# Last steps of a sequence spread over the loop in two attention layers, and a product moved on GpSimd in a state-space layer

## The chip, the cores and the metric

The kernel runs on one core of a Trainium2 chip. Its time is device time in microseconds (us) of one execution of the whole program. Before the change the median of three runs is 2588.48 us (2585.68 to 2595.79). The engines are named as in the profile: PE is TensorE's matrix multiplication and PEld its weight loads, DVE is VectorE, ACT is ScalarE, POOL is GpSimd, SP is SyncE, which here only issues transfers.

## The reference, cut to what matters

A decoder of four layers works on x of shape (16, 128, 256): 16 sequences of 128 rows with 256 features. Each layer adds an attention (or state-space) step, a cross attention to a context, and a feed-forward step, each on the layer-normalised x. The change touches three of the twelve steps:

```python
# layer 1, cross attention: heads are groups of features, q and k are normalised along the features
qn = _l2norm(qh, axis=-2); kn = _l2norm(kh, axis=-2)            # 8 heads of 16 features, 256 "positions"
sm = jax.nn.softmax(5.0 * jnp.einsum('bhdq,bhdk->bhqk', qn, kn), axis=-1)
out = jnp.einsum('bhqk,bhdk->bhdq', sm, vh).reshape(B, Dv, Tq)

# layer 2, state-space in chunks of 32 steps, 32 heads of 16, state 128
y = (Y_diag + Y_off).reshape(b, nc * CHUNK, HEADS, HEAD_DIM) + D[None, None, :, None] * xs
y = y * silu(gate); y = y * rsqrt(mean(y * y) + EPS) * norm_w
return y @ out_proj_w.T

# layer 3, attention: 16 heads of 16, causal with a bias that falls with the distance
attn = jax.nn.softmax(q @ k / 4 + alibi, axis=-1)
return (attn @ v) @ Wo.T

# in the decoder
x = x + _L1_xattn_ref(_layernorm(x), ctx, ctx)
x = x + _L2_attn_ref(_layernorm(x), ...)
x = x + _L3_attn_ref(_layernorm(x), ...)
```

## The kernel before

x stays in on-chip memory for the whole program. The 16 sequences are worked through in four groups of four (g is the group, j the sequence in it, b = 4g + j). Instructions are written in Python in the order of the loops, and a scheduler then orders them on each engine by their dependences and its own estimate of times; each engine works through its own list strictly in that order. The order in the text is therefore a wish and not the order on the engines. `issue_after(i)` forbids the scheduler to put the instructions of its block ahead of instruction i on i's engine.

PSUM, where TensorE writes, is divided into three pools of 512-column buffers: four for scores and projections (`psum`), two for transposes and the like (`psum_t`), two for accumulated results (`psum_a`). A buffer is free again when its last reader is done.

**Layer 1 cross attention** (L693 to L834). `unit(g)` prepares a group in steps: norms (pn, L737), their square roots, and for each sequence a spread of them over the rows (pb, L750) from which qn, kn and the masked queries qb are made. `attend` goes through a group's sequences, each in two half steps (e = 0, 1). A half step makes eight score products ps (L769), each of 32 rows, so that four of them stand in different row groups of TensorE; they are recorded as sixteen. Four exponentials on ScalarE (L775) follow. The product with the values, `mix` (L784), is put off by one half step through the list `late`, so that it doesn't wait for the exponentials. After the second half step's `mix`, `close` ends the sequence in one go: oT is copied out of PSUM (L802, VectorE), turned by four transposes pqT (L807), the reciprocal of the sums rd (L810) and the weighted o (L814) are made on VectorE, two transposes poT (L821) turn it back, and it is added to x (L157). Between half steps one step of the next group's `unit` is issued, and two pieces of `ternary`, which rounds layer 2's feed-forward weights on VectorE (L1468 to L1491) and has no other relation to this step. These pieces stand behind the latest copy of oT by `issue_after`.

**Layer 2 state-space** (`mamba` with `blocks`). For every sequence `begin` transposes the convolved input xc into px (L1110) and copies it to xs, alternately by ScalarE (L89) and VectorE (L91). GpSimd then multiplies xc in place by the skip's factor D (L1113), and makes three scaled copies xw of xs (L1141) for the products poff (L1147), from which yo (L1149) comes. `parts` makes xdp on GpSimd (L1157), transposes yo (pyo, L1161), adds it to the scaled xc (L1163), and makes the products py (L1176) with mt (L1169). `gate` (L1192 to L1197) multiplies by the gate and sums squares; `out` (L1205 to L1209) normalises and projects. GpSimd's queue holds L1113, L1141, L1157, L1193, L1196, L1197 and L1205 of neighbouring sequences.

**Layer 3 attention** (L1530 to L1645). Per sequence: four scores ps (L1584), to each a bias (L1588) and the negative maximum (L1592) on VectorE, the subtraction on GpSimd (L1593), the exponential on ScalarE (L1594). `mix`, one sequence later through `late`, transposes the sixteen heads' weights (ppT, L1602), copies them (L1604) and multiplies with the values (po, L1609), and copies the result to oT (L1614). `close`, one sequence after that through `later`, transposes oT (pqT, L1626), divides by the sums (rd L1629, o L1631), transposes o (pt, L250), copies it (oo, L89 and L91), multiplies with Wo (pa, L97) and adds it to x (L157).

Of the kernel before, what the change touches and what calls it, by code (L numbers as in the profile page):

```python
# [17 lines left out]
ALU = mybir.AluOpType  # L18
# [4 lines left out]
P = 128  # L23
NB = 16
S = 128
# [16 lines left out]
class Decoder:  # L42
# [86 lines left out]
    class Pipe:  # L129
# [8 lines left out]
        def step(self):  # L138
            for d in self.due:
                d[0] -= 1  # L140
            now = [w for n, w in self.due if n <= 0]
            self.due = [d for d in self.due if d[0] > 0]
            for w in now:
                w()
# [548 lines left out]
    def L1_xattn(self):  # L693
        nc = self.nc
        H, d = 8, 16
        with ExitStack() as es:
# [58 lines left out]
                    yield  # L755

            late, units, copies = [], {}, []
            ternary = self.ternary_parts(tn)

            def attend(g, ahead):  # L760
                v, kn, qb = units.pop(g)
                for j in range(GB):
                    b, state = g * GB + j, {}
                    for e in range(2):
                        ps = [self.psum("ps") for r in range(4)]
                        for c in range(2):
                            for r in range(4):
                                rw = slice(32 * r, 32 * r + 32)
                                nc.tensor.matmul(  # L769
                                    ps[r][:, D * c : D * c + D], kn[rw, j, self.cols(c)], qb[rw, j, e], start=True, stop=True  # L770
                                )
                        got = []
                        for r in range(4):
                            pT = big.tile([P, 2, D], F32, tag="pT", name="pT")
                            nc.scalar.activation(pT.rearrange("p c t -> p (c t)"), ps[r], AF.Exp, scale=5.0)  # L775
                            got.append(pT)

                        def mix(j=j, b=b, e=e, got=got, state=state, v=v):
                            if e == 0:
                                state["po"] = self.psum_a("po")  # L780
                            po = state["po"]
                            for c in range(2):
                                for r in range(4):
                                    nc.tensor.matmul(  # L784
                                        po[32 * r : 32 * r + 32, D * e : D * e + D], v[:, j, c, 2 * r + e, :],
                                        got[r][:, c, :], start=(c == 0), stop=(c == 1),
                                    )
                            if e == 1:
                                close(b, po)

                        for f in late:
                            f()
                        late[:] = [mix]
                        next(ahead, None)
                        if copies:
                            with self.tc.issue_after(copies[-1].ins):
                                for _ in range(2):
                                    next(ternary, None)

            def close(b, po):  # L800
                oT = sm.tile([P, 512], F32, tag="oT", name="oT")
                copies.append(nc.vector.tensor_copy(oT, po))  # L802
                pt = self.psum_t("pqT")
                for a in range(2):
                    for e in range(2):
                        at = D * e + P * a
                        nc.tensor.transpose(pt[:, self.cols(2 * a + e)], oT[:, at : at + P], self.ident)  # L807
                pv = pt.rearrange("p (n x) -> p n x", x=32)
                rd = sm.tile([P, 2 * H], F32, tag="rd", name="rd")
                nc.vector.reciprocal(rd, pv[:, :, d])  # L810
                o = sm.tile([P, 2, P], F32, tag="o", name="o")
                for a in range(2):
                    ar = slice(H * a, H * a + H)
                    nc.vector.tensor_tensor(  # L814
                        o[:, a].rearrange("p (r e d) -> p e r d", r=4, e=2),
                        pv[:, ar, 0:d].rearrange("p (e r) d -> p e r d", e=2),
                        rd[:, ar].rearrange("p (e r) -> p e r", e=2).unsqueeze(3).broadcast_to([P, 2, 4, d]), ALU.mult,
                    )
                pb = self.psum_t("poT")
                for a in range(2):  # L820
                    nc.tensor.transpose(pb[:, self.cols(a)], o[:, a, :], self.ident)  # L821
                self.add_x(b, pb[:, :D])
# [3 lines left out]
            for g in range(NG):  # L826
                ahead = unit(g + 1) if g + 1 < NG else iter(())
                attend(g, ahead)
                for _ in ahead:
                    pass  # L830
            for f in late:
                f()
            for _ in ternary:
                pass  # L834

# [126 lines left out]
    def mamba(self, L, H, N, clip):  # L962
# [3 lines left out]
        nc = self.nc  # L966
        HD, Q = 512 // H, 32
        blocks = H == 32
# [8 lines left out]
        with ExitStack() as es:  # L977
# [128 lines left out]
            def begin(g, j, bc_, sz, xc, dt, a, xy):  # L1106
                b = g * GB + j
                pt = self.psum_t("px")
                for c in range(4):
                    nc.tensor.transpose(pt[:, self.cols(c)], xc[:, c, j, :], self.ident)  # L1110
                xs = sm.tile([P, 512], F32, tag="xs", name="xs")
                self.evac(xs, pt)
                nc.gpsimd.tensor_tensor(  # L1113
                    xc[:, :, j, :], xc[:, :, j, :], nw[:, 1, :].unsqueeze(2).broadcast_to([P, 4, S]), ALU.mult
                )
                pg = self.psum_t("pg")
                nc.tensor.matmul(pg[:, :P], bc_[:N, 0, self.cols(j)], bc_[:N, 1, self.cols(j)], start=True, stop=True)
                gm = sm.tile([P, P], F32, tag="gm", name="gm")
                nc.vector.tensor_tensor(gm, pg[:, :P], upto, ALU.mult)
                dj = dt[:, j, :].unsqueeze(2).broadcast_to([P, H, HD])  # L1120
                lcs = []
                if (g, j) not in steps_of:
                    steps(g, j)
                for rb in steps_of.pop((g, j)):
                    ps = self.psum("pseg")
                    nc.tensor.matmul(ps, after, rb.rearrange("p h l -> p (h l)"), start=True, stop=True)
                    lc = ps if blocks else big.tile([P, 512], F32, tag="lc", name="lc")
                    nc.scalar.activation(lc, ps, AF.Exp)
                    lcs.append(lc.rearrange("p (h l) -> p h l", h=per))
                if not blocks:  # L1130
                    xd = sm.tile([P, 512], F32, tag="xd", name="xd")
                    nc.gpsimd.tensor_tensor(heads(xd), heads(xs), dj, ALU.mult)
                    pipe.put(2, lambda: whole(g, j, gm, lcs[0], xd, sz, xc))
                    return lambda: None
                xd = xds[b % 2]
                gf = sm.tile([P, P], F32, tag="gf", name="gf")
                nc.vector.tensor_tensor(gf, pg[:, :P], prior, ALU.mult)
                pf, n, xws = self.psum("poff"), 3 * Q, []
                for c in range(3):
                    xw = big.tile([P, 512], F32, tag="xw", name="xw", bufs=4)  # L1140
                    nc.gpsimd.tensor_tensor(  # L1141
                        heads(xw)[:n], heads(xs)[:n], xy[:n, c, j, :].unsqueeze(2).broadcast_to([n, H, HD]), ALU.mult
                    )
                    xws.append(xw)
                for c in range(4):
                    to = slice(Q * c, Q * c + Q)
                    nc.tensor.matmul(pf[to], gf[:n, to], xws[max(c - 1, 0)][:n], start=True, stop=True)  # L1147
                yo = sm.tile([P, 512], F32, tag="yo", name="yo")
                nc.vector.tensor_tensor(  # L1149
                    heads(yo), heads(pf), xy[:, 3, j, :].unsqueeze(2).broadcast_to([P, H, HD]), ALU.mult  # L1150
                )
                return lambda: parts(g, j, gm, lcs, xd, dj, yo, xs, sz, xc)
# [377 lines left out]
    def L3_attn(self):  # L1530
        nc = self.nc
# [3 lines left out]
        with ExitStack() as es:  # L1535
# [87 lines left out]
            def close(b, oT):  # L1623
                pt = self.psum_t("pqT")
                for n in range(4):
# [6 lines left out]
                    o.rearrange("p (r n d) -> p n r d", r=4, n=4), pv[:, :, 0:d].rearrange("p (n r) d -> p n r d", n=4),  # L1632
                    rd.rearrange("p (n r) -> p n r", n=4).unsqueeze(3).broadcast_to([P, 4, 4, d]), ALU.mult,
                )
                oo = sm.tile([P, 2, P], F32, tag="oo", name="oo")
                self.transpose_rows(oo, [o])
                pa = self.psum_a()
# [1 line left out]
                self.add_x(b, pa[:, :D])  # L1639

            self.overlap(NG, project, attend)
            for q in (later, late, later):
                for f in list(q):
                    q.remove(f)
                    f()  # L1645
# [375 lines left out]
```

## Time and profile before

| what | value |
|---|---|
| median of three runs | 2588.48 us |
| the profiled execution | 2586.49 us, its span 2584.8 us |
| layer 1 cross attention, about 733 to 903.5 us of the span | 170.5 us |
| layer 2 state-space, about 1087 to 1391 us | 304 us |
| layer 3 attention, about 1926 to 2128 us | 202 us |
| scores of layer 1's cross attention, L769, 512 records | 85.4 us busy |
| exponentials there, L775, 128 | 67.6 us busy, 601 ns each |
| skip's product, L1113, 32 in both state-space layers | 33.8 us busy, 1057 ns each |
| subtraction of the maxima in layer 3, L1593, 64 | 65.2 us busy, 1038 ns each |

A record of the profile is one instruction on one engine with its start and length; a matmul on 4-byte numbers is recorded as two. "Idle before, releaser" names what the engine waited for. The granted clock is the share of TensorE's full clock that it had in a stretch; in this profile it is 0.50 or 1.00 at any moment, and a mean over a longer window lies between. Neighbouring matmuls overlap, so the busy time of a line is the time that its records cover together.

### The profile page before, as it was taken

The numbers are of one execution on the slowest core, as the hardware profiler recorded it, in microseconds if no ns is written. First come the engines' busy times: TensorE is split into PE (matmuls) and PEld (weight loads), VectorE is DVE, ScalarE is ACT, GpSimd is POOL, SyncE is SP. The second block draws the span as 40 slices with busy tenths as digits, with TensorE's granted clock in tenths as the row PEclk, the third lists the DMA queues.
The fourth block names the chain that finished last, engine by engine and source line by source line (L and its number), as shares of the span: only waits on it lengthen the run. The fifth ranks groups of instructions, "written<-read, shape, count | busy, mean of one in ns | idle before, by whom it ended". The sixth has DMA issues, their size and how long they took to land. (4 is left out here: it accounts for less than half of the span.)

```text
span 2584.8 us, 33315 instructions
## 1 busy us (share of the span) xinstructions
PE 2283.6 (88%) x12494; PEld 1419.7 (55%) x12510; DVE 1589.0 (61%) x3395; ACT 956.2 (37%) x1726; POOL 949.5 (37%) x983
## 2 busy tenths in 40 slices
PE   7889899889988989989889799898888987699998
PEld 4654454446644445644445465564555555577776
DVE  7996865476756687778887666664465556211110
ACT  1124545355444423344332433345434442112121
POOL 5720102223431142144546866746443333112122
PEclk9987879999977899989889999999999997899999
DMA  4000010000111000100010000000000002233221
GB/s 137 1 29 26 21 58 6 1 25 3 40 41 33 24 1 3 44 1 1 1 29 8 1 1 5 29 34 1 1 29 1 15 32 89 97 87 99 64 71 19
DMA packets 61086, 77.79 MB, mean 30 GB/s; under 512 B 8851, under 2 KB 50579, under 8 KB 60820
## 3 DMA queue, kind: packets, MB, share of 16 engines
q1 hardware_dynamic: 53604, 66.57, 8.0%
q0 software_dynamic: 6784, 8.48, 1.9%
q8 instruction: 101, 1.65, 0.3%
q14 instruction: 69, 0.57, 0.1%
q10 hardware_dynamic: 528, 0.52, 0.1%
HBM read 56.88 MB, written 18.67 MB: 29 GB/s over the span
## 5 line engine op out<-in xcount | busy, mean ns | idle before, releaser
L1897 POOL DMA_INDIRECT out_dram<-y,to x40 | 60.9, 1523 | 301.5 <-ACT y L1896 301.5
L1888 DVE TENSOR_TENSOR hT<-sl,pgb 128x288 f32<-128x288 f32 x112 | 50.6, 454 | 147.7 <-PE pgb L97 147.6
L97 PE MATMUL pga<-xeT,e_w1T 128*128 128x288 f32 x448 | 128.3, 409 | 0.0
L97 PE MATMUL pgb<-xeT,e_w3T 128*128 128x288 f32 x448 | 127.2, 407 | 1.0 <-DVE hT L1888 1.0
L97 PE MATMUL pa<-e_w2T,hT 128*128 128x256 f32 (+1 forms) x560 | 124.5, 380 | 0.0
L97 PEld LDWEIGHTS pa<-e_w2T,hT 128*128 128x128 f32 (+1 forms) x560 | 99.2, 179 | 22.1 <-issue 3.0
L1593 POOL TENSOR_TENSOR sc<-sc,mx 128x512 f32<-128x512 f32 x64 | 65.2, 1038 | 121.7 <-DVE mx L1592 79.5
L1887 ACT ACTIVATE sl<-pga 128x288 f32<-128x288 f32 x112 | 45.9, 410 | 168.5 <-PE pga L97 168.4
L1357 ACT ACTIVATE sc<-sc 128x512 f32<-128x512 f32 x64 | 40.3, 630 | 165.5 <-POOL sc L1356 165.5
L775 ACT ACTIVATE pT<-ps 128x512 f32<-128x512 f32 x128 | 67.6, 601 | 90.0 <-PE ps L769 86.1
L97 PEld LDWEIGHTS pgb<-xeT,e_w3T 128*128 128x128 f32 x448 | 84.9, 190 | 25.2 <-DVE hT L1888 2.0
L214 DVE TENSOR_SCALAR xn<-x,mv,rs 128x256 f32<-128x256 f32 x176 | 86.0, 533 | 20.6 <-POOL rs L107 20.6
L97 PEld LDWEIGHTS pga<-xeT,e_w1T 128*128 128x128 f32 x448 | 84.8, 191 | 23.4
L419 PE MATMUL ps<-qb,kT 32*128 32x512 f32 x256 | 90.6, 795 | 7.8 <-ACT pT L424 4.7
L618 POOL TENSOR_TENSOR rest<-h,h 128x512 f32<-128x512 f32 (+1 forms) x56 | 66.0, 1180 | 74.2 <-ACT h L617 71.8
L201 POOL COPY rs<-mv 128x4 f32<-128x4 f32 x46 | 10.1, 219 | 223.5 <-DVE mv L199 215.7
L424 ACT ACTIVATE pT<-ps 128x512 f32<-128x512 f32 x128 | 68.2, 605 | 61.8 <-PE ps L419 61.7
L1113 POOL TENSOR_TENSOR xc<-xc,nw 128x512 f32<-128x512 f32 x32 | 33.8, 1057 | 153.5 <-PE px L1110 133.9
L198 DVE BATCH_NORM_STATS2 st<-x 128x6 f32<-128x256 f32 x192 | 78.1, 414 | 16.9 <-POOL x L461 10.1
L461 POOL TENSOR_TENSOR x<-x,o 128x256 f32<-128x256 f32 x16 | 16.4, 1028 | 194.7 <-DVE o L457 194.7
L769 PE MATMUL ps<-qb,kn 32*128 32x256 f32 x512 | 85.4, 522 | 1.7 <-ACT pT L775 1.7
L622 DVE TENSOR_TENSOR h<-rest,h 128x512 bf16<-128x512 f32 (+1 forms) x56 | 40.5, 724 | 75.1 <-ACT h L621 75.1
(499 smaller groups left out, 6075.0 us busy)
## 6 DMA issues: line engine op xcount, KB each, us to landing
e_w1T<-in_L_w1T SPq DMA_DIRECT2D x8, 896.0 KB, 6.2
e_w3T<-in_L_w3T SPq DMA_DIRECT2D x8, 896.0 KB
e_w2T<-in_L_w2T SPq DMA_DIRECT2D x8, 896.0 KB
xe<-slots SPq DMA_DIRECT2D x8, 652.5 KB
slots<-blank SPq DMA_DIRECT2D x6, 783.0 KB, 12.7
x<-in_x SPq DMA_DIRECT2D x4, 512.0 KB
ctx<-in_ctx SPq DMA_DIRECT2D x16, 128.0 KB
raw<-in_L_wgu SPq DMA_DIRECT2D x4, 512.0 KB
```

The costliest lines, as they stand in the source:

```text
L97: self.nc.tensor.matmul(out, a, b, start=(i == 0), stop=(i == n - 1))
L198: nc.vector.bn_stats(st[:, j, :], self.x[:, g * GB + j, :])
L214: nc.vector.tensor_scalar(xn[:, j, :], self.x[:, g * GB + j, :], mv[:, j, 0:1], rs[:, j : j + 1], ALU.subtract, ALU.mult)
L419: nc.tensor.matmul(ps[r], kT[rw, j, c, :], qb[rw, j, c].rearrange("p e n -> p (e n)"), start=True, stop=True)
L424: nc.scalar.activation(pT.rearrange("p e n -> p (e n)"), ps[r], AF.Exp, scale=d**-0.5)
L618: engines[0].tensor_tensor(r, t, a, ALU.subtract)
L769: nc.tensor.matmul(ps[r][:, D * c : D * c + D], kn[rw, j, self.cols(c)], qb[rw, j, e], start=True, stop=True)
L775: nc.scalar.activation(pT.rearrange("p c t -> p (c t)"), ps[r], AF.Exp, scale=5.0)
L1593: nc.gpsimd.tensor_tensor(sc, sc, mx.unsqueeze(2).broadcast_to([P, 4, S]), ALU.add)
L1887: nc.scalar.activation(sl, pa[:, :HALF], AF.Silu)
L1888: nc.vector.tensor_tensor(hT[:, f, hs], sl, pb[:, :HALF], ALU.mult)
L1897: i = nc.gpsimd.indirect_dma_start(out, bass.IndirectOffsetOnAxis(to[:m, t : t + 1], 0), y[:m], None, bounds_check=NB * S - 1, oob_is_err= ...
```

## The change

In layer 1's cross attention `close` is cut into three. It now only copies oT and puts `weigh` (pqT, rd, o) into `late`, which puts `turn` (poT and the sum into x) into `late` in its turn. `late` is emptied once in each half step by `step`, which runs only what was there when it began; so the three parts are issued in three half steps following each other. At the end `step` is called until the list is empty.

In layer 3's attention `close` is cut in two in the same way: `expand` (the transposes of o, the product with Wo and the sum into x) goes into `later` and is issued one sequence later. The last emptying of the lists has one round more.

In layer 2's state-space step the product with the skip's factor becomes a function `skip`. With `blocks` (layer 2) it is issued after the three xw, and `issue_after` forbids the scheduler to put it ahead of the third. Layer 1's state-space step issues it where it stood.

```diff
@@ layer 1 cross attention
             late, units, copies = [], {}, []
+
+            def step():
+                for f in list(late):
+                    late.remove(f)
+                    f()
+
@@
-                        for f in late:
-                            f()
-                        late[:] = [mix]
+                        step()
+                        late.append(mix)
                         next(ahead, None)
@@ def close(b, po)
                 oT = sm.tile([P, 512], F32, tag="oT", name="oT")
                 copies.append(nc.vector.tensor_copy(oT, po))
+                late.append(lambda: weigh(b, oT))
+
+            def weigh(b, oT):
                 pt = self.psum_t("pqT")
...
+                late.append(lambda: turn(b, o))
+
+            def turn(b, o):
                 pb = self.psum_t("poT")
...
-            for f in late:
-                f()
+            while late:
+                step()
@@ state-space, begin
-                nc.gpsimd.tensor_tensor(
-                    xc[:, :, j, :], xc[:, :, j, :], nw[:, 1, :].unsqueeze(2).broadcast_to([P, 4, S]), ALU.mult
-                )
+                def skip():
+                    nc.gpsimd.tensor_tensor(
+                        xc[:, :, j, :], xc[:, :, j, :], nw[:, 1, :].unsqueeze(2).broadcast_to([P, 4, S]), ALU.mult
+                    )
+
+                if not blocks:
+                    skip()
@@
-                    nc.gpsimd.tensor_tensor(
+                    last = nc.gpsimd.tensor_tensor(
                         heads(xw)[:n], heads(xs)[:n], xy[:n, c, j, :].unsqueeze(2).broadcast_to([n, H, HD]), ALU.mult
                     )
                     xws.append(xw)
+                with self.tc.issue_after(last.ins):
+                    skip()
@@ layer 3 attention, close
+                later.append(lambda: expand(b, o))
+
+            def expand(b, o):
                 oo = sm.tile([P, 2, P], F32, tag="oo", name="oo")
                 self.transpose_rows(oo, [o])
...
-            for q in (later, late, later):
+            for q in (later, late, later, later):
```

## The prediction

> **What bounds the kernel now.** I read the page first, then sums by window for the three stages that the change touches, then windows laid on the clock's own steps, the order of time inside one sequence, and the waits by stage. The page gives TensorE as the busiest engine, and its clock row is not flat:
>
> ```profile
> PE 2283.6 (88%) x12494; PEld 1419.7 (55%) x12510; DVE 1589.0 (61%) x3395; ACT 956.2 (37%) x1726; POOL 949.5 (37%) x983
> ...
> PEclk9987879999977899989889999999999997899999
> ```
>
> The three stages, in columns of window, length, busy time of PE, PEld, DVE, ACT and POOL, granted clock, DMA share and GB/s:
>
> ```profile
> 733.00:903.50 170.50, 155.53 (x1174) 78.22 (x1173) 110.10 (x232) 80.83 (x141) 23.44 (x29) 0.77 0.10 34
> 1087.00:1391.00 304.00, 261.31 (x1818) 136.74 (x1820) 243.71 (x455) 115.78 (x167) 144.17 (x170) 0.92 0.03 8
> 1926.00:2128.00 202.00, 176.90 (x1140) 102.10 (x1141) 121.15 (x247) 96.40 (x176) 70.04 (x78) 0.94 0.03 11
> ```
>
> Layer 1's cross attention (the first) keeps TensorE busy 91% of the time, but at 0.77 of its clock; the other two have 0.92 and 0.94. What idle does there is seen in windows of the clock's own step, 3.41 us (length, PE busy, granted clock):
>
> ```profile
> 753.73:757.15 3.42, 3.14 (x36) 1.00 0.00 0
> 757.15:760.56 3.41, 2.35 (x22) 1.00 0.00 0
> 760.56:763.97 3.41, 3.41 (x25) 0.50 0.02 5
> ...
> 842.48:845.89 3.41, 2.41 (x29) 1.00 0.00 1
> 845.89:849.30 3.41, 3.41 (x17) 0.50 0.39 126
> ```
>
> A window with 3.14 us of work keeps the clock at 1.00; one with 2.35 or 2.41 (69 to 71%) is followed by half the clock. In this stage the six drops to half follow windows busy 0.69 to 0.78 of their length; every window above 0.8 held the clock, and three below 0.8 did too. So a hole of 1 us costs itself, and then windows at half speed: 78.8 of the 170.5 us run at 0.50 with no hole in them (78.3 busy), and 91.7 us at 1.00 with 14.5 us of holes. Inside one sequence:
>
> ```profile
> 812.73 1.07 PE L784 MATMUL po<-pT,va 128*32 128x256 f32 x16
> 813.73 0.70 PE L769 MATMUL ps<-qb,kn 32*128 32x256 f32 x4
> 814.61 0.66 PE L807 MATMUL pqT<-ident,oT 128*128 128x128 f32 x4 [0.18 <-DVE oT L802]
> 815.20 0.71 PE L769 MATMUL ps<-qb,kn 32*128 32x256 f32 x8
> 816.67 0.33 PE L821 MATMUL poT<-ident,o 128*128 128x128 f32 x1 [0.76 <-DVE o L814]
> ```
>
> The ends of a sequence (pqT, poT) stand inside the next scores, each waiting for VectorE, and they cut the sixteen score records into pieces. The waits, stage by stage (us, times, longest):
>
> ```profile
> PE poT L821 <- DVE o L814: 8.0, 11, 1.1
> PE pqT L807 <- DVE oT L802: 5.2, 10, 1.5
> ...
> POOL xw L1141 <- DVE xs L91: 24.8, 8, 4.0
> PE poff L1147 <- POOL xw L1141: 19.2, 16, 2.4
> ...
> PE pa L97 <- ACT oo L89: 6.2, 15, 1.3
> PE pqT L1626 <- ACT oT L1614: 5.3, 5, 1.3
> ```
>
> **Layer 1 cross attention.** No instruction is added or removed. In the built program's order a half step becomes "16 score records, pqT or poT, 16 po records, at times one pb". So oT has the whole next scores as cover (1.15 us in one piece, where the clock is full) against a copy of 0.69, and o has pqT to poT, 1.07 + 1.15 us and 0.55 more with a pb, against rd 0.25 and o 0.48.
> (a) Holes: 8.0 + 5.2 = 13.2, less the last sequence's 0.78 + 0.77, which has nothing to stand behind: 11.7. What is late next is VectorE's queue: in the new order up to four pieces of the ternary work (L1481, L1483, L1485, L1487: 0.68 + 0.69 + 0.65 + 1.22 = 3.2) lie between oT and rd, so o comes 3.2 + 0.7 after oT, and poT's place about 3.0 to 3.5 after it. That gives back 0 to 0.9 us in the 12 sequences with ternary work; I take 0.4, about 5. Left: -7.
> (b) Pieces: a half step with its scores cut took 0.98 + 0.71 + 0.70 in the last group, whole 1.15. Not all of the 1.24 is won, since scores also wait for their four buffers: the exponentials' bursts follow each other no closer than 3.2 us (878.68 to 881.86). Two of these are 6.4 against 7.2 measured from oT to oT (879.67, 886.97, 894.11), and 0.5 of the 0.8 is hole, counted in (a). 0.3 x 16: -5; bounds 0 and, by the pieces, -16.
> (c) Clock: the first 10.5 us at half speed (733 to 743.5) come before any end of a sequence and stay. Of the other 68.3, each microsecond avoided saves half. Bounds: all avoided, -34; and above nothing, if the clock comes back less often (last rival). In the last group the clock held for 34 us although holes of 0.5 remained, and windows will have about 0.3 us of hole per half step; but the holes of (a) don't all go. I take 40% avoided: -13.7.
> Sum -26. VectorE's 110.1 us busy is a floor far below 144.
> The Trainium skill, "TensorE: Matmul & The Clock Gate", Part 1, has the same step (3413 ns, free-running) but says the clock halves only after a whole idle window, and advises against holes over some 3 us. The trace differs: the longest hole in this stage is 1.45 us (780.00 to 781.46), and there are six drops. By that rule of the Trainium skill (c) is nothing, and the sum is -12 - 1 - 6.
>
> **Layer 2 state-space.** Sixteen products on POOL of 1.04 us (L1113) go from ahead of the three xw to behind them; TensorE's, VectorE's, ScalarE's and SP's orders stay. Where VectorE copies xs (8 times) the product lay inside the 24.8 us that POOL waited for xs: nothing is won, and xdp comes 1.04 later, up to 2.3 with the sz and rms steps now ahead of it; py starts 1.7 to 12.8 us after xdp, so at most 0.6 is felt once. The product's reader, the sum at L1163, comes at least 2.5 us after xw, behind poff, yo and pyo. Where ScalarE copies xs, xw starts 0.4 earlier (once 1.1), but poff was waiting for xw in three of these. -1; bounds -5 (0.4 to 1.1 everywhere) and +3 (each late xdp felt by 0.4).
>
> **Layer 3 attention.** The steps from oo to x go one sequence later; 16 x (two pt, four pa records, two copies, one sum) move, none is added. TensorE's holes here: pa 6.4, pt 6.0, pqT 5.3, as the idle before them, 17.7. The last sequence keeps about 2.6, since its chain is as long as before. A sequence in the middle takes 9.6 us with 0.5 of hole at pa and ppT, so it is mainly the group ends that gain. Now pt waits for nothing, pqT stands behind pt and one score, pa behind three pqT; but VectorE's copy of oo now stands between a score's sum (L1588) and its maximum (L1592), and holds up that maximum, POOL's subtraction and the exponential if pt is late. I take 40%: -6; bounds -15 and, with 0.3 lost per sequence, +5. The clock (22.6 us at half) I leave.
>
> **Sum.** -26 - 1 - 6 = -33. The profiled execution took 2586.5 (span 2584.8 and 1.7 around it), 2.0 below the median shown; 2553.5 there is 2555.5 as a median.
>
> **The rivals.**
> 1. The clock holds throughout: (c) is -34. For it: the last group, 34 us at 1.00. Against: pb and pn fill single row groups there, and other groups have them. 2588.5 - 46 - 7 = 2535.
> 2. VectorE sets the pace: 110 us of work in some 140 leaves little, and rd and o stand behind ternary pieces as before; holes move from pqT to poT, the clock goes on as it is. Layer 1 -4, the rest nothing: 2584.
> 3. Holes go, but the clock falls and rises at the same places as before, since its drops would come from something else than the holes: layer 1 -12, the rest -7: 2569.5. For it: windows at 0.68, 0.70 and 0.75 held the clock. This is also what the rule of the Trainium skill told above would give.
> 4. Slower: after a drop the clock does not come back. At half clock it rose only after windows almost wholly of ps and po (740.1, 787.9, 832.2 from their start); windows with a pqT or poT in them stayed at half (767.4, 784.5, 859.5). Now a transpose stands in every half step, so such windows get rare. A sequence at half is 4.16 + 3.88 + 1.81 and 1.0 for pb and pn, 10.85, so 10.5 + 16 x 10.85 = 184; by the slow sequences of before (13.4 with pb from 846.8 to 860.2, 11.1 without), less 1 for pieces, 200. Middle +22, less 7 elsewhere: 2604. It decides from the point where nearly all of the stage is at half speed; against it, drops should get rare too.
> The Trainium skill, "TensorE: Matmul & The Clock Gate", Part 4, speaks for this one: it says that transposes don't count as busy for the gate. The trace agrees with it at 767.4, 784.5 and 859.5.
>
> **How the numbers follow.** Forecast 0.50 (own range 2540 to 2573), rival 1 0.15, rival 2 0.13, rival 3 0.10, rival 4 0.12. Predicted 2556. The range takes in the first rival and most of the second's and fourth's spread: 2533 to 2592, with some 0.18 left out. What tells from no change is about 0.5%, 13 us. Faster: 0.50 + 0.15 + 0.10, all but a little: 0.74. Within: rival 2 and the lower edge of rival 4: 0.15. Slower: 0.11.
>
> **What would show it.** Layer 1's stage near 145 us, with a clock above 0.85 and less than 5 us of PE idle before pqT and poT; oT to oT below 7 us where the clock is full. The idle before pt, pa and pqT in layer 3 near 10 us, its stage near 196. Layer 2's within 5 us of 304. The forecast is wrong if the clock of layer 1's stage stays at 0.77 or falls, if holes stand before poT as long as now, or if layer 3's maxima wait for the copy of oo.

## The result, and the profile after

The changed kernel takes 2549.4 us (median of four runs, 2542.98 to 2557.13) against 2588.91 (four runs, 2585.68 to 2595.79): a ratio of 0.9862, with a 95% interval of 0.9829 to 0.9895. The profiled execution took 2542.98 us, its span 2541.2; that of before had 2584.8. All stage lengths here and below are of one profiled execution of each kernel, which for the changed kernel was the fastest of its four (2543 to 2557 us, at a mean clock of 0.933 to 0.925; measured again, the fastest of five) and for the kernel before lay near its median, so the differences lean in favour of the change. The page's rows of busy time and of the granted clock:

```profile
PE 2237.3 (88%) x12510; PEld 1400.4 (55%) x12510; DVE 1603.6 (63%) x3395; ACT 952.0 (37%) x1726; POOL 950.6 (37%) x983
...
PEclk9997879999989999988999999999999996899999
```

TensorE has the same work and is busy 46 us less, at a higher clock. The three stages, summed over windows (length, busy time of PE, PEld, DVE, ACT and POOL, granted clock, DMA share, GB/s):

```profile
731.00:874.50 143.50, 119.32 (x1175) 67.19 (x1174) 115.81 (x232) 79.35 (x141) 24.65 (x31) 0.88 0.13 41
1069.00:1355.50 286.50, 244.69 (x1790) 128.19 (x1792) 239.28 (x435) 109.10 (x156) 140.98 (x168) 0.93 0.03 9
1890.00:2082.00 192.00, 176.23 (x1148) 99.32 (x1148) 124.02 (x250) 94.76 (x177) 70.86 (x79) 0.96 0.04 11
```

Layer 1's cross attention went from 0.77 of the clock to 0.88. Cut at the same records in both traces, the stretches are, in us:

| stretch | before | after | difference |
|---|---|---|---|
| up to layer 1's first score | 732.8 | 731.1 | -1.7 |
| layer 1 cross attention, first score to last poT | 170.3 | 143.0 | -27.3 |
| to layer 2's first poff (unchanged code) | 195.7 | 195.1 | -0.6 |
| layer 2 state-space, first poff to last sum into x | 291.4 | 286.0 | -5.4 |
| to layer 3's first score (unchanged code) | 535.6 | 534.9 | -0.7 |
| layer 3 attention, first score to last pa | 201.0 | 190.1 | -10.9 |
| to the end (unchanged code) | 457.9 | 461.0 | +3.1 |

The differences of each stretch look as if every part had won. The waits of TensorE say something else (us in total, times, longest; lines of the changed kernel are up to 20 higher than those of before):

```profile
PE poT L832 <- DVE o L822: 13.6, 9, 4.3
...
PE pqT L815 <- DVE oT L807: 6.1, 4, 2.2
...
PE ps L775 <- ACT pT L781: 4.3, 3, 2.1
```

Layer 1's holes did not shrink. The idle before poT rose from 8.0 to 13.8 us, that before pqT from 5.2 to 6.1, and all of TensorE's idle in the stage from 15.0 to 24.2. What grew is seen on VectorE around the longest hole (start, us, operation):

```profile
843.74 0.66 DVE L807 COPY oT<-po 128x512 f32<-128x512 f32 x1
844.32 0.68 DVE L1508 TENSOR_TENSOR tn_q<-tn_q,tn_w 128x1024 bf16<-128x1024 bf16 x1
845.03 0.69 DVE L1485 CAST tn_w<-raw 128x1024 bf16<-128x1024 f32 x1
845.76 1.22 DVE L1488 TENSOR_REDUCE tn_sc<-tn_w 128x16 f32<-128x1024 bf16 x1
...
849.74 1.23 DVE L1495 TENSOR_TENSOR tn_q<-tn_w,tn_sc 128x1024 bf16<-128x1024 bf16 x1 [2.05 <-DMA tern<-tn_q]
850.88 0.25 DVE L818 RECIPROCAL rd<-pqT 128x16 f32<-128x16 f32 x1
851.16 0.49 DVE L822 TENSOR_TENSOR o<-pqT,rd 128x128 f32<-128x128 f32 x2
```

pqT was done at 845.1, but rd stands behind a whole row of ternary pieces in VectorE's queue, one of which even waits 2.05 us for the transfer that still reads tn_q. o came at about 851.5, and TensorE stood for 4.32 us before poT.

For each stage I use one more measure. I count a microsecond of TensorE at half clock as half a microsecond's work, so the length of a stage is its work at full clock, plus its holes, plus half of its half-clock time (summed from the clock's records). This is a rough measure: sixteen po take 1.07 us at full clock and 1.94 at half, a little less than twice as long, and "work" is the time that TensorE's records cover, with whatever holds up a row of them inside (sixteen scores last 1.15 to 2.50 us at full clock). Layer 1's 170.3 was 116.1 + 15.0 + 39.4, and the 143.0 is 102.0 + 24.2 + 17.2 (to 0.4, since some idle falls into half-clock time).

### The profile page after: what moved, and what is told of

It reads as the page before. It is cut to its first block, busy times and chain, and to the rows that moved or that the text cites. A ratio compares the mean times of both kernels' runs of the same rounds, so it can differ in the third digit from the quotient of the medians.

```text
span 2541.2 us, 33355 instructions
## 1 busy us (share of the span) xinstructions
PE 2237.3 (88%) x12510; PEld 1400.4 (55%) x12510; DVE 1603.6 (63%) x3395; ACT 952.0 (37%) x1726; POOL 950.6 (37%) x983
## 5 line engine op out<-in xcount | busy, mean ns | idle before, releaser
L97 PEld LDWEIGHTS pa<-e_w2T,hT 128*128 128x128 f32 (+1 forms) x560 | 99.2, 179 | 22.1 <-issue 3.0
L1610 POOL TENSOR_TENSOR sc<-sc,mx 128x512 f32<-128x512 f32 x64 | 65.9, 1038 | 118.2 <-DVE mx L1609 101.1
L1156 POOL TENSOR_TENSOR xw<-xs,xy 96x512 f32<-96x512 f32 x48 | 51.6, 1094 | 116.1 <-DVE xs L91 67.9
L1373 POOL TENSOR_TENSOR sc<-sc,mx 128x512 f32<-128x512 f32 x64 | 66.1, 1038 | 55.6 <-DVE sums L1377 44.0
## 6 DMA issues: line engine op xcount, KB each, us to landing
slots<-blank SPq DMA_DIRECT2D x6, 783.0 KB, 13.7
```

The source lines that it names most:

```text
L97: self.nc.tensor.matmul(out, a, b, start=(i == 0), stop=(i == n - 1))
L1156: last = nc.gpsimd.tensor_tensor(heads(xw)[:n], heads(xs)[:n], xy[:n, c, j, :].unsqueeze(2).broadcast_to([n, H, HD]), ALU.mult)
L1373: nc.gpsimd.tensor_tensor(sc, sc, mx.unsqueeze(2).broadcast_to([P, 4, S]), ALU.add)
L1610: nc.gpsimd.tensor_tensor(sc, sc, mx.unsqueeze(2).broadcast_to([P, 4, S]), ALU.add)
```

## The experiments

The table gives layer 1's stage for each kernel that moves it, from its one profiled execution: its length, half-clock time, TensorE's holes (those before poT, pqT and ps in brackets), and its work at full clock. The kernel before was measured again beside each set of runs, with medians of 2576.9, 2585.3 and 2580.4 us; the ratios are against those, so that kernels of different sets compare by their ratios rather than by their medians.

| kernel | length | half clock | holes | work |
|---|---|---|---|---|
| before | 170.3 | 78.9 | 15.0 (8.0, 5.2, 1.7) | 116.1 |
| changed | 143.0 | 34.4 | 24.2 (13.8, 6.1, 4.3) | 102.0 |
| changed, measured again | 139.8 | 31.0 | 22.1 (11.7, 6.1, 4.3) | 102.2 |
| layer 1's part alone | 145.0 | 44.8 | 21.3 (13.0, 4.0, 4.3) | 102.3 |
| only pqT later | 169.4 | 68.3 | 23.6 (17.4, 0.8, 5.4) | 111.9 |
| only poT later | 140.3 | 30.6 | 14.9 (5.6, 8.6, 0.7) | 110.8 |
| pieces behind o | 146.8 | 48.0 | 20.3 (0.8, 14.4, 5.1) | 102.8 |
| pieces spread | 133.3 | 20.3 | 17.7 (0.8, 11.2, 5.4) | 105.4 |
| pieces after the stage | 127.6 | 27.5 | 9.4 (0.8, 3.2, 5.4) | 104.4 |
| filler of 32 rows | 160.0 | 17.1 | 6.0 (4.0, 2.0, 0) | 145.5 |
| filler of 128 rows | 156.2 | 6.9 | 6.5 (4.6, 1.9, 0) | 146.2 |

**Layer 1's part alone.** The kernel before with the new layer 1 cross attention.

> The kernel before with the layer 1 cross attention part of the change alone. Theory (the part acts in its own stage: whole scores and fewer windows at half clock, against larger holes): first score to last poT 143 us +- 6 (170.3 before, 143.0 after), layer 2 state-space 291 and layer 3 attention 201 as before; time about 27 below before, 2561. Rival (the clock's falls depend on where the stage happens to stand against the 3.41 us grid, so the gain is one execution's luck): stage anywhere between 150 and 170 with half-clock time above 50 us, time 2570 to 2585.

Median 2556.3 us, 0.9931 of before (0.9905 to 0.9958): some 18 us, less than expected, though the stage came out as said. Layer 2 took 286.7 us with code that this version leaves as it was, where 291 was expected. That is the first sign that layer 2's 5 us were not the change's.

**Layer 3's part alone.**

> The kernel before with the layer 3 attention part alone. Theory (the later steps fill TensorE's holes before pt, pqT and, through the clock, save a little more): first score to last pa 190 us +- 3 (201.0 before, 190.1 after), idle before pt under 2 us (6.0 before), before pa about 8 (6.4 before); time 8 to 11 below before. Rival (the 11 us were the clock's state on entry, carried over from the other parts): stage 196 to 201, half-clock time in it 20 us or more, time within 5 of before.

The stage is 191.1 us, the idle before pt 1.0 and before pa 8.2, as the theory said. The time is not told apart from before: 2569.8 us, a ratio of 0.9994 (0.9969 to 1.0018), with runs from 2562 to 2588. In the ten profiled executions with the new layer 3 its stage takes 190.1 to 191.2, in the four with the old one 199.2 to 201.2; the gain of 9 to 10 us is there each time, but is smaller than what the rest of the kernel varies by. Layer 2, unchanged here too, took 282.9. The two parts' ratios multiply to 0.9925, while the changed kernel has 0.9862 and, measured again, 0.9895; given the intervals, whether the parts add up to the whole stays open.

**Ternary pieces behind o.**

```diff
-                copies.append(nc.vector.tensor_copy(oT, po))
+                nc.vector.tensor_copy(oT, po)
@@ weigh, behind the two products o
+                copies.append(last)
```

> The changed kernel, with layer 1's ternary pieces released behind the last o of a sequence instead of behind its copy oT. Theory (the holes before poT come from ternary pieces that lie between oT and rd on VectorE): idle before poT falls from 13.8 to under 5 us, stage from 143 to 130 to 136, half-clock time from 34 to under 25; time 2537 to 2545 against a median of 2549 for the changed kernel. Rival (VectorE has no room for four pieces in a half step, so x, oT and with them pqT are late instead): idle before pqT grows from 6.1 to over 11, stage 140 to 150, time unchanged.

The rival held: 0.8 us before poT, but 14.4 before pqT, stage 146.8, median 2547.1 (ratio 0.9888, 0.9843 to 0.9932). The pieces make the holes, and what stands behind them on VectorE is late: with the pieces behind oT it is rd and o, with the pieces behind o it is the sum into x and with it the next oT.

**Pieces spread.** As above, but copies of oT are kept in the list as well, so that two pieces follow oT and two follow o.

> The changed kernel, with ternary pieces released two behind oT and two behind o. Theory: with two pieces (about 1.6 us) a half step neither rd nor oT is late; idle before poT and pqT together falls from 19.9 to under 8, stage 126 to 134, half-clock time under 20; time 2535 to 2545. Rival (holes are set by the order of the rows' products and roots, not by the ternary pieces): idle before poT and pqT stays above 15, stage 140 to 146, time unchanged at 2549.

The stage is 133.3 us with 20.3 at half clock. The two waits fell from 19.9 to 12.0, not to under 8. The median is 2543.4 (0.9890, 0.9859 to 0.9920). In the profiled execution the ten microseconds don't show in the span, since the stage began 12 us later, at 743.3: the earlier layers, in unchanged code, had 164 us at half clock against 140.

**The changed kernel again.**

> The changed kernel once more, unedited, for a second look at the same code. Theory (the layer 1 and layer 3 gains belong to the change, layer 2's 5 us to the clock): layer 1 cross attention 143 +- 7, layer 3 attention 190 +- 2, and layer 2 state-space anywhere from 283 to 291, with its holes at 41 to 42 us as in the first look (38 before). Rival (the first profiled execution was an unusually good one): layer 1 stage above 152.

Layer 1 139.8, layer 3 190.1, layer 2 289.1 with holes of 41.4: the theory's numbers. Median 2555.7, ratio 0.9895 (0.9834 to 0.9956).

**Pieces spread, layer 2 as before.** The kernel with spread pieces, and the layer 2 part of the change undone.

> The changed kernel with the ternary pieces two behind oT and two behind o, and without layer 2's move (its product ahead of the scaled rows again). Theory (in layer 2 the move trades 1.5 us of hole before poff for 3.6 before pyo, and the rest was clock): layer 2 holes 37 to 39 with under 1 before pyo, layer 2 at 264.5 to 266 us in time at full clock against 266 to 269 with the move; layer 1 stage about 133 as with pieces spread, total 2 to 3 below that kernel. Rival (the move does win, by 5): layer 2 at 288 or more, total 3 to 5 above.

Layer 1's stage took 135.6 us, the median is 2540.4 (0.9840, 0.9776 to 0.9903). Layer 2 has holes of 39.1 us with under 1 before pyo, and is 266.1 long at full clock, both sizes 0.1 above the ranges given. The total is not told apart from the version with spread pieces. Over all profiled executions, seven with the old order (two of them the filler kernels) have 264.5 to 266.1, mean 265.5, and seven with the new one 265.8 to 269.0, mean 267.6; their holes are 37.2 to 39.1 and 41.4 to 42.3. The lengths as they stand, 282.9 to 291.4 and 284.2 to 289.1, tell nothing, because the half-clock time there varies from 31 to 51 us. So by this measure the move costs about 2 us of that stage, too little to be seen in the kernel's time. Where from is seen in VectorE's groups of that stage (busy, mean ns), of before and of the changed kernel:

```profile
L1098 DVE TENSOR_TENSOR rb<-upto,a 128x512 f32<-128x512 f32 x28 | 36.5, 1332 | 2.3 <-PE pseg L1126 2.2
```

```profile
L1109 DVE TENSOR_TENSOR rb<-upto,a 128x512 f32<-128x512 f32 x28 | 43.0, 1567 | 1.6 <-PE pseg L1141 1.5
```

The same 28 products take 6.5 us longer. In the changed kernel 8 of them lie beside the moved product on GpSimd and take 17.9 us together; in the kernel before none does. A single one lasts 0.68 us when GpSimd is still (10 of the 28, in both kernels) and up to 3.20 us before and 3.72 after beside GpSimd. yo stands behind them, so pyo waits: its hole is 0.6 us before and 4.3 after. In the changed kernel, GpSimd first, then VectorE:

```profile
1218.10 3.09 POOL L1156 TENSOR_TENSOR xw<-xs,xy 96x512 f32<-96x512 f32 x3 [12.87 <-DVE mt L1186]
1221.15 1.48 POOL L1125 TENSOR_TENSOR xc<-xc,nw 128x512 f32<-128x512 f32 x1
1222.60 1.21 POOL L1174 TENSOR_TENSOR xdp<-xs,dt 128x256 f32<-128x256 f32 x2
```

```profile
1221.66 0.68 DVE L1209 TENSOR_TENSOR xc<-xc,py 128x512 f32<-128x512 f32 x1
1222.26 2.10 DVE L1109 TENSOR_TENSOR rb<-upto,a 128x512 f32<-128x512 f32 x1
1224.28 0.68 DVE L1186 TENSOR_TENSOR mt<-pseg,gm 128x512 f32<-128x512 f32 x1
1224.88 0.68 DVE L1166 TENSOR_TENSOR yo<-poff,xy 128x512 f32<-128x512 f32 x1
```

rb lies beside the moved product (L1125) and xdp and takes 2.10 us in place of 0.68. The Trainium skill, "SBUF — State Buffer", section "SBUF: two separate sides", says that a VectorE operation with two inputs in SBUF and a GpSimd operation that reads SBUF shut each other out for a whole instruction; rb has two inputs in SBUF, the on-chip memory in which x lies too, and the trace agrees. mt and yo, with one input in PSUM, keep their 0.68.

**Pieces after the stage.** No ternary piece is issued in the loop; all follow the last sequence.

```diff
-                                for _ in range(2):
-                                    next(ternary, None)
+                                pass
```

> The changed kernel with layer 1's ternary pieces left until the last sequence is done. Theory (VectorE, loaded with ternary pieces, sets the pace of the stage's first three groups and makes the holes): idle before poT and pqT together under 8 (19.9 in the changed kernel), half-clock time under 25 (34), first score to last poT 115 to 128; the pieces then cost some 45 us of VectorE behind the stage, so the time is 5 to 25 above the changed kernel. Rival (the holes come from the roots, the norms and ScalarE's order, not from ternary work): idle above 14, stage 138 or more.

The waits before poT and pqT, in the table of waits of this kernel:

```profile
PE ps L775 <- ACT pT L781: 5.4, 3, 2.1
PE pqT L814 <- DVE oT L806: 3.2, 4, 1.2
PE pb L750 <- DVE kn L753: 0.9, 1, 0.9
PE poT L831 <- DVE o L821: 0.8, 1, 0.8
```

4.0 us are left of the 19.9, so the pieces made nearly all of them. The half-clock time, 27.5, missed its mark of 25 by a little. And no cost of the pieces shows behind the stage, against what was expected: the stretch to layer 2 is as long as with them (195.1), and the median, 2545.7 (0.9857, 0.9796 to 0.9918), is not above the changed kernel's by ratio (0.9895 in the same set).

**Only pqT later**, then **only poT later**: `weigh` calls `turn` at once, or `close` calls `weigh` at once.

```diff
-                late.append(lambda: turn(b, o))
+                turn(b, o)
```

> The changed kernel, where poT follows o at once again and only pqT comes one half step later. Theory (the two transposes cut the scores in two places, and each cut costs alike): stage between the two kernels, 152 to 160, idle before poT 6 to 9, work at full clock 107 to 111 (116.4 before, 102.3 after). Rival (pqT's delay is the whole gain): stage 143 +- 4. Second rival (only both together help, since the windows stay cut): stage 165 or more.

The second rival's length held: 169.4 us, at 0.80 of the clock, 17.4 of idle before poT, median 2573.1 (0.9961, 0.9926 to 0.9997). Its work at full clock, 111.9, fell by about 4 from the kernel before (the expectation's 116.4 and 102.3 are the table's 116.1 and 102.0). The stage's window in this kernel, columns as in the three windows above:

```profile
742.37:912.19 169.82, 146.24 (x1175) 76.78 (x1174) 116.92 (x232) 79.76 (x141) 23.70 (x30) 0.80 0.10 34
```

> The changed kernel, where pqT follows oT at once again and poT comes one half step later. Theory (a half step must hold its scores in one piece and its po behind them, or the clock stays low for longer): stage 150 to 170, half-clock time 50 us or more, as with only pqT delayed (169.4 and 68). Rival (what costs in that other version is the 17.4 us of holes before poT, which this order lacks): stage 140 to 148.

The rival held here as well: 140.3 us, median of two runs 2547.5 (0.9867, 0.9823 to 0.9912), no worse than the whole change. The same window of this kernel:

```profile
741.00:881.79 140.79, 125.91 (x1175) 69.70 (x1174) 111.95 (x232) 79.21 (x141) 23.71 (x30) 0.89 0.12 41
```

So putting off poT by itself has the gain in these executions. Putting off pqT too makes the scores whole (work 102 in place of 111) and gives the same back in holes (24 in place of 15).

**Filler of 32 and of 128 rows.** The kernel before, with four products per sequence on a constant tile `fill`, two ahead of pqT and two ahead of poT; K is 32 or 128.

```diff
+                for _ in range(2):
+                    nc.tensor.matmul(pt[:, 0:D], self.ident[:K], fill[:K], start=True, stop=True)
```

> The kernel before with two more products of 32 rows (32*128, 32x256, of a constant tile) ahead of each sequence's pqT and two ahead of its poT, into the same bank, overwritten by the transposes: added work, no other result. Theory (the clock falls after windows that hold little full-row work, whatever their busy share): the same windows fall, half-clock time stays at 70 us or more (78.9 before). Rival (the clock falls by idle alone, and filled holes keep it): half-clock time under 50, alike with 32 and with 128 rows.

> As the version with products of 32 rows, but with all 128 rows (128*128, 128x256): same places, same number. Theory (full-row work in each window keeps the clock): half-clock time under 40 us, at least 30 below the version with 32 rows, and the stage shorter than with 32 rows by half of that. Rival (idle alone decides): half-clock time and stage within 10 us of the version with 32 rows.

The theory's number for 32 rows was wrong by far: 17.1 us at half clock, not 70. With the holes filled, the clock keeps up with few rows too. The stage's window with 32 rows, and then with 128, in the same columns:

```profile
742.05:902.49 160.44, 154.46 (x1303) 89.37 (x1302) 109.84 (x232) 79.64 (x141) 21.53 (x27) 0.95 0.11 36
```

```profile
735.36:891.99 156.63, 150.11 (x1303) 87.30 (x1302) 109.73 (x232) 79.64 (x141) 21.44 (x27) 0.98 0.11 36
```

With 128 rows only what was inherited at the stage's start is left at half clock, 6.9 us, but 10 us between the two, two falls of the clock against none, settle nothing about rows. What is settled is odd enough: about 30 us of useless work at full clock made the stage 10 to 14 us shorter than before. As a median the 128-row kernel takes 2562.6 (0.9930, 0.9902 to 0.9958), the 32-row one 2583.2 (0.9994, 0.9971 to 1.0018), the same as before within its interval: with 32 rows the stage's gain does not show in the kernel's time.

**The parts that won.** Layers 1 and 3 changed, layer 2 as before, the pieces after the stage.

> Layers 1 and 3 changed, layer 2 as before, and the ternary pieces left until layer 1's last sequence is done. Theory (the three findings add up): layer 1 stage 126 to 130 with VectorE busy 67 there, layer 2 holes 38 to 39, layer 3 stage 190 to 191, median 2530 to 2542, 2 to 5 below the version with spread pieces and layer 2 as before. Rival (the late pieces cost behind the stage what the stage wins): median 2545 or more.

2540.8 us (0.9837, 0.9803 to 0.9872). The findings add up to the stage lengths expected (127.6, 191.1, layer 2's holes 37.9), and this version and the one with spread pieces, at 2540.4 (0.9840, 0.9776 to 0.9903), have the lowest ratios. The 2 to 5 us expected between the two do not show. They are not told apart from each other, nor, by these intervals, from the changed kernel.

## Why the prediction was right, and where it was not

2556 was predicted, and 2549.4 and, measured again, 2555.7 came out. The mechanism that was meant to carry most of the gain did: layer 1's stage, its clock from 0.77 to 0.88. But its 145 us came true by luck: the terms were +9.2, -14.1 and -22.3 where -7, -5 and -13.7 were forecast, two mis-sized and one of the wrong sign, and their errors cancelled. Two of the prediction's own signs of being wrong were seen as well: the holes before poT are longer than before, and in layer 3 maxima waited for the copy of oo.

- **(a) Holes, -7: wrong in sign.** They grew by 9.2 (7.1 when measured again). The step that failed is "That gives back 0 to 0.9 us in the 12 sequences with ternary work; I take 0.4, about 5". The mechanism was named rightly, pieces between oT and rd, but it was costed with the pieces at their bare lengths and nothing else between. The trace shows pieces of 1.42 in place of 0.69, the next group's four xn (2.57 together) and the roots' reciprocal (3.35) in the same queue, and the wait of 2.05 for a transfer. Without the pieces the two waits are 4.0 us, 9.2 less than before, against the 11.7 that the working had ahead of its 5 for the pieces; the scores' wait for the exponentials, which it did not count, grew from 1.7 to 5.4 in that kernel.
- **(b) Whole scores, -5: too small.** The work at full clock fell by 14.1, close to the bound of -16; the time that the score records cover, counted in the same way, went from 63.2 to 52.1. (The bound was mis-added: sixteen times 1.24 is 19.8.) Of the two rows at hand, 1.24 per half step by the scores' pieces and 0.8 per two by the distance from oT to oT, the second was taken, and the first was nearer.
- **(c) Clock, -13.7: too small.** Half of 78.9 less 34.4 is 22.3. Of the 68.3 us that could go, 41 went (60%, with 40% taken). But the reason given, fewer holes, is not what happened. Falls in the stage went only from six to five. What changed most is how soon the clock came back: after the first score the stretches at half were 17.1, 10.2, 6.8, 3.4, 6.8 and 23.9 us before, and 6.8, 3.4, 6.8, 3.4 and 6.8 after.
- **Layer 2, -1 within -5 to +3: about +2.** The five microseconds won in the two traces were the clock's. The wait before poff fell by 1.6, about as forecast, and that before pyo grew by 3.7: missing from the working was that the moved product would lie beside rb on VectorE.
- **Layer 3, -6: -9 to -11.** The three holes that were costed fell by 5.3 us (pa 6.4 to 8.4, pt 6.0 to 1.0, pqT 5.3 to 3.0), much as forecast. Not counted were ppT, ps and po, another 4.1 together, and the clock, whose half time fell from 21.5 to 13.7. The feared wait of the maxima behind oo's copy came twice, with a small price: in twelve sequences the copy stands between a score's sum and its maximum, and in two of them it waited 0.60 us for pt, so that the maximum began 0.8 us after the sum in place of 0.1. The first of the two:

```profile
1946.90 0.69 DVE L1605 TENSOR_TENSOR sc<-ps,bias 128x512 f32<-128x512 f32 x1 [0.58 <-PE ps L1601]
1948.18 0.29 DVE L91 COPY oo<-pt 128x128 f32<-128x128 f32 x1 [0.60 <-PE pt L250]
1948.39 0.68 DVE L1609 TENSOR_REDUCE mx<-sc 128x4 f32<-128x512 f32 x1
```

Of the rivals, the first (the clock holds throughout) and the third (it falls and rises where it did) are out with 34.4 us at half clock, where they had 10.5 and 78.9. The second was half right: VectorE's queue does move holes from one transpose to the other, but the clock improved all the same. The fourth fell on its premise, since windows with transposes in them did bring the clock back. In these windows of the changed kernel (start and end, length, TensorE's busy time and records, granted clock, DMA share, GB/s) the third holds two poT, at its own clock of 0.50; the one behind it had 1.00:

```profile
768.92:772.34 3.42, 2.49 (x34) 1.00 0.49 138
772.34:775.76 3.42, 1.37 (x20) 1.00 0.32 111
775.76:779.17 3.41, 3.41 (x30) 0.50 0.00 0
...
806.47:809.89 3.42, 1.85 (x28) 1.00 0.22 90
809.89:813.30 3.41, 2.06 (x32) 1.00 0.00 0
813.30:816.71 3.41, 2.75 (x34) 1.00 0.02 5
```

The same lines show that some holes cost less than before: 1.37 us of work in a window (40%) lost the clock, but 1.85 and 2.06 (54 and 60%) kept it, where the kernel before lost it at 69 to 78%. Others did not: the windows from 782.58 and 820.13, busy 50 and 56%, lost it. I laid the clock's steps of 3.41 us on TensorE's records of this stage in twelve profiled executions (the fillers left out; several follow the same course, so the counts are not independent). Of the windows at full clock (a record counts where it starts):

| busy share | few po (under 8 records) | a run of po (8 or more) |
|---|---|---|
| under 0.45 | 13 of 13 fell | 13 of 13 fell |
| 0.45 to 0.90 | 28 of 57 fell | 8 of 77 fell |
| over 0.90 | 0 of 3 fell | 0 of 203 fell |

The old order, with pqT, poT and their waits strung through one half step's scores, makes more windows with hardly any po, and over all kernels these fall at shares at which others mostly hold. The new order puts a run of sixteen po into each half step. But this covers only a part of it: of the six falls before the change, three came after windows with sixteen po (69 to 71% busy), and with only poT put off, seven windows of 0.45 to 0.90 with few po lost the clock only once. It is read off, too, not shown: the fillers, which were to show that the rows of the products decide, were not able to, and whether it is rows, the kind of the products or the place of the hole in a window stays open. So does what brings the clock back: all 72 returns came out of windows at half clock that were at least 94% busy, but about as many such windows, some 70, did not bring it back.

The Trainium skill's rule that a whole idle window is needed ("TensorE: Matmul & The Clock Gate", Part 1) would have left the clock as it was, the third rival's 2569.5, and does not hold here: of the changed kernel's five falls in the stage only one follows a window without any work (847.44 to 850.85). The same page of the Trainium skill, section "A second HAM failure mode: psum-queue depth-cycling", which tells of a clock that swings through short idle between groups of matmuls, is the one that the trace agrees with, as far as the swing goes: the six falls before the change follow windows whose longest hole was 0.58 to 1.06 us (1.45 with the part of it that lies behind the window's edge). The cause that it names was not tried here.

## What to carry to other kernels

A step put off until its input is ready only pays if the engine that makes the input is not filled with other work in between: look at what the scheduler or the text has queued there, with its waits, before counting the hole as gone. Where the clock takes part, compare stages by work, holes and half-clock time apart, over several executions; the difference of two stage lengths gave layer 2 a gain of 5 us, where its length at full clock had a loss of about 2. A product moved to an idle stretch of GpSimd is not free if VectorE reads two operands from on-chip memory in that stretch.

## What the runs showed of the hardware that was not expected

- Unchanged code varies by more than layer 3's whole gain: the layers up to layer 1's first score took 727.5 to 744.6 us in fourteen profiled executions, with 126 to 164 us at half clock (659 to 671 us less half of that).
- A stage with more work can take less time. Products that compute nothing, in its holes, raised its clock from 0.77 to 0.95 and 0.98 and made it 10 and 14 us shorter, though of the two kernels only the one with 128 rows was faster as a whole, by 0.7%.
- A VectorE product with both operands in on-chip memory took 0.68 us alone and up to 3.72 beside GpSimd.
